# One quad of maxima in place of two, with its logits computed once and lowered by pixel between two turns

## The chip, the cores and the metric

The kernel runs on one core of one Trainium2 chip. The metric is the device time of one execution, in microseconds (us); a figure for a kernel is the median of its runs.

TensorE does matmuls, VectorE and GpSimd elementwise work, ScalarE exponentials and copies; DMA queues move data. PSUM is the memory that TensorE writes. This kernel uses it in tiles of two banks, called pairs, and three pairs rotate.

## The reference, cut to what matters

```python
def amm_conv3x3(x, centroids, w_sub, stride=1):          # a 3x3 convolution by code book
    p = ...                                                # (B, pixels, C, 9) patches
    d = sum(p*p) - 2.0 * einsum('bncs,cks->bnck', p, centroids) + sum(centroids**2)
    attn = softmax(-d, axis=-1)                            # over k = 16 codes of one channel
    lut = einsum('cks,cso->cko', centroids, w_sub)
    return einsum('bnck,cko->bno', attn, lut)
```

This runs twice for each of 16 images of 256 channels and 28 x 28 pixels. Group norm comes before it, batch norm and a squeeze-excite gate around it. A softmax doesn't change if the same number is taken from all 16 logits of a channel and pixel, and both kernels use this to keep the exponentials in range.

## The kernel before

The work of a layer and image is cut into 2 tiles of pixels (384 and 400) and 8 quads of 32 channels, so 16 slots. In each slot a group of **logits** (patches times codes), a group of **numerators** (exponentials times codes) and some **look-ups** (normalised numerators times weights, a full 128 x 128 matmul each) go to TensorE. Logits and numerators use small matmuls, 32 x 32 tiles of the array:

```python
def logits(u, rows):
    l, n = u["l"], u["px"][1]
    ps = [pair(), pair()]
    for t in range(4):
        for i in range(4):
            c = 32 * ctile(i, t)                     # (i + t) % 4
            nc.tensor.matmul(ps[t // 2][c : c + 32, t % 2, :n],
                lhsT=wd[l][32 * i : 32 * i + rows, 4 * u["m"] + t, :],
                rhs=u["pt"][32 * i : 32 * i + rows, t, :n], start=True, stop=True)
    return ps
```

The 16 matmuls (each leaves two records in the trace, 32 in all) go to 16 different tiles. Those of t = 0, 1 fill the first pair, those of t = 2, 3 the second. These are the two halves of a group.

The quads are sorted by how large their logits can get. In layer 2, quads 0 and 4 (`MAXED`) need the true maximum over the codes. They compute logits once to find it, then again with the maximum taken off. To turn means to transpose here; in the profile it is STREAM_TRANSPOSE:

```python
def a_turn(u):           # logits out of PSUM, turned so that codes lie along the free axis
    ...
def a_max(u, v):         # VectorE: maximum over 16 codes
    ...
def m_turn(u): ...       # turn the maxima, write them to DRAM (m_out), read them back as rows (m_in)
def b_logits(u):         # the logits again, with the maxima as more rows of the patches
    u["lg"] = logits(u, MROW + NCH if u["maxed"] else ONE + 1)
```

Each kernel is emitted in an order fixed by slot and position, and every engine works through its own part in that order. The positions within a slot:

```python
LOGITS, LOAD, MOVE, EXP, LOOK_A, NUM, TURN, SMALL, LOOK_B, MAX, LOOK_C, TURN_BACK, REST = range(13)
```

After the numerators VectorE turns them out of PSUM (`b_turn`) and takes the reciprocal, GpSimd normalises (`c_scale`), and VectorE turns the result back as `q` for the look-ups (`c_turn`, in TURN_BACK). A guard at the end checks the sums of exponentials and redoes the batch in a safe way if they leave a range.

## Time and profile before

| | before |
|---|---|
| time, median of 4 runs | 2812.78 us (2810.43 to 2818.25) |
| profiled execution | 2814.8 us, mean granted clock 0.990 |
| TensorE busy | 98% |
| VectorE / GpSimd / ScalarE busy | 80% / 63% / 39% |
| a round: a layer 1 and a layer 2 image, 32 slots | 169.21 us |

A busy share of 98% means less than it seems, since ends of matmuls are modelled. So I account for TensorE by starts: the time from the first record of a group to the start of the next thing. Over ten rounds in the middle of the run, per round:

| us per round | logits | numerators | look-ups | small matmuls | sum |
|---|---|---|---|---|---|
| before | 31.50 (36 groups) | 28.26 (32) | 108.18 | 1.28 | 169.21 |

### The profile page before, as it was taken

What the parts mean: (1) busy time and instruction counts of PE and PEld (TensorE: products, weight loads), DVE (VectorE), ACT (ScalarE), POOL (GpSimd) and SP (SyncE); (2) the same over time, 40 slices, a digit from 0 to 9 for tenths busy, and PEclk for the clock granted to TensorE, in tenths of its full rate; (3) what the DMA queues carried; (4) which work ended last, traced back from release to release, by engine and by line L of the source; (5) the groups of instructions that cost most, each with busy time, mean ns of one, the idle gap of its engine ahead of it and who ended that gap; (6) DMA issues with size and microseconds to landing.
All of it is one profiled execution on the core that took longest, in us unless ns stands there. A gap on an engine that the chain in (4) does not pass through costs nothing.

```text
span 2814.8 us, 94692 instructions
## 1 busy us (share of the span) xinstructions
PE 2756.0 (98%) x39794; PEld 1090.2 (39%) x39794; DVE 2252.0 (80%) x2772; ACT 1086.5 (39%) x1595; POOL 1782.1 (63%) x2589
## 2 busy tenths in 40 slices
PE   6999999999999999999999999999999999999996
PEld 3333333333333343333333333343333334333332
DVE  4668788887878878788887878878788887878885
ACT  2333433434334343433434334343433434334332
POOL 3785666756666575665756667575665756665653
PEclk9999999999999999999999999999999999999998
DMA  8787878768687676777777687676777767674641
GB/s 223 205 202 193 234 204 225 194 169 219 155 226 195 167 212 165 214 184 191 191 175 218 159 222 195 169 214 161 215 189 191 190 170 221 161 210 106 163 122 55
DMA packets 292787, 525.83 MB, mean 187 GB/s; under 512 B 94096, under 2 KB 247552, under 8 KB 292352
## 3 DMA queue, kind: packets, MB, share of 16 engines
q0 software_dynamic: 51808, 269.48, 36.0%
q1 hardware_dynamic: 240544, 250.20, 34.5%
q8 instruction: 315, 5.16, 0.8%
q14 instruction: 120, 0.98, 0.1%
HBM read 267.87 MB, written 251.69 MB: 185 GB/s over the span
## 4 chain that ended last, share of the span: by engine, by line
PE 92%; DVE 3%; POOL 2%; DMA 2%; issue 1%; ACT 0%; SPq 0%; DVEq 0%; POOLq 0%; ACTq 0%
PE acc L717 58%; PE pair L585 17%; PE pair L653 15%; DVE nt L665 1%; POOL k L681 1%; DMA pt<-pat 1%; DVE q L699 0%; DMA pat<-side 0%; DVE rc L671 0%; PE pair L319 0%; DMA out_dram<-y 0%; POOL pat L486 0%; PE pair L514 0%; POOL total L693 0%; DVE gn_st L434 0%
## 5 line engine op out<-in xcount | busy, mean ns | idle before, releaser
L717 PE MATMUL acc<-q,ws 128*128 128x384 f32 (+1 forms) x4096 | 1645.9, 520 | 5.1 <-ACT y L739 2.8
L681 POOL TENSOR_TENSOR k<-nt,rc 128x832 f32<-128x832 f32 (+1 forms) x512 | 802.9, 1568 | 980.6 <-DVE rc L671 970.7
L665 DVE STREAM_TRANSPOSE nt<-pair 128x832 f32<-128x832 f32 (+1 forms) x1024 | 979.3, 994 | 487.3 <-PE pair L653 436.0
L643 ACT ACTIVATE e<-pair 128x800 f32<-128x800 f32 (+1 forms) x1024 | 787.5, 821 | 1356.8 <-PE pair L585 1303.2
L717 PEld LDWEIGHTS acc<-q,ws 128*128 128x128 f32 x4096 | 698.1, 190 | 903.2 <-issue 577.6
L585 PE MATMUL pair<-pt,wd 19*32 19x384 f32 (+2 forms) x18432 | 556.6, 501 | 11.4 <-DMA pt<-pat 8.2
L699 DVE STREAM_TRANSPOSE q<-k 128x832 f32<-128x832 f32 (+1 forms) x512 | 488.9, 955 | 0.8 <-POOL k L681 0.8
L653 PE MATMUL pair<-e,cw 32*32 32x384 f32 (+1 forms) x16384 | 485.5, 501 | 0.3 <-DVE nt L665 0.2
L671 DVE RECIPROCAL rc<-nt 128x104 f32<-128x104 f32 (+1 forms) x512 | 398.5, 778 | 17.6
L585 PEld LDWEIGHTS pair<-pt,wd 19*32 19x32 f32 (+1 forms) x18432 | 138.2, 103 | 339.8 <-issue 276.2
L687 POOL TENSOR_TENSOR tail<-nt,rc 128x104 f32<-128x104 f32 (+1 forms) x512 | 236.7, 462 | 0.0
L653 PEld LDWEIGHTS pair<-e,cw 32*32 32x32 f32 x16384 | 119.9, 103 | 289.5 <-issue 154.8
L717 PE MATMUL acc<-qt,ws 128*128 128x400 f32 (+1 forms) x512 | 219.3, 510 | 0.0
L693 POOL TENSOR_TENSOR total<-total,nt 128x96 f32<-128x96 f32 (+1 forms) x448 | 197.4, 441 | 0.0
L486 POOL DMA_DIRECT2D pat<-side x274 | 184.7, 674 | 3.5 <-ACT side L475 3.0
L693 POOL TENSOR_TENSOR total<-total,rc 128x96 f32<-128x96 f32 (+1 forms) x448 | 176.1, 393 | 0.0
L717 PEld LDWEIGHTS acc<-qt,ws 128*128 128x128 f32 x512 | 91.1, 190 | 100.1 <-issue 50.3
L609 DVE TENSOR_REDUCE mx<-z 128x48 f32<-128x768 f32 (+1 forms) x128 | 120.6, 942 | 0.0
L604 DVE STREAM_TRANSPOSE z<-pair 128x768 f32<-128x768 f32 (+1 forms) x128 | 118.1, 961 | 0.0
L486 POOL DMA_DIRECT2D pat<-im x136 | 92.0, 677 | 0.7 <-ACT side L475 0.6
L739 ACT ACTIVATE y<-acc,bnsh,bnsc 128x384 f32<-128x384 f32 (+1 forms) x64 | 43.3, 677 | 87.3 <-PE acc L717 81.6
L551 POOL TENSOR_TENSOR y<-y,xt 128x392 f32<-128x392 f32 x60 | 65.9, 1099 | 10.4 <-ACT y L547 10.4
(113 smaller groups left out, 720.5 us busy)
## 6 DMA issues: line engine op xcount, KB each, us to landing
pat<-side POOLq DMA_DIRECT2D x232, 588.0 KB, 6.0
pt<-pat SPq DMA_DIRECT2D x1024, 112.5 KB
pt<-pat SPq DMA_DIRECT2D x1024, 108.0 KB
pat<-im POOLq DMA_DIRECT2D x116, 588.0 KB, 5.9
xt<-in_x POOLq DMA_DIRECT2D x32, 784.0 KB, 8.1
out_dram<-y POOLq DMA_DIRECT2D x16, 784.0 KB, 6.1
pat<-side POOLq DMA_DIRECT2D x24, 300.0 KB, 5.3
pat<-side POOLq DMA_DIRECT2D x18, 288.0 KB, 5.5
```

Source lines behind the costliest of these rows:

```text
L486: eng.dma_start(view(pat, (ROWS * p0 + 9 * k + 3 * dx) * HW + px, [[ROWS * HW, m], [HW, 3], [1, n]]), bass.AP(v.tensor, v.offset, [list(v. ...
L585: nc.tensor.matmul(ps[t // 2][c : c + 32, t % 2, :n], lhsT=wd[l][32 * i : 32 * i + rows, 4 * u["m"] + t, :], rhs=u["pt"][32 * i : 32 * i + ...
L609: nc.vector.tensor_reduce(u["mx"][:, 2 * v : 2 * v + 2].rearrange("p t (j b) -> p t b j", j=2)[:, :, :nb], u["z"].pop(0)[:, : 64 * nb].rea ...
L643: nc.scalar.activation(e[:, :, :n], ps[:, :, :n], AF.Exp, scale=2.0)
L653: nc.tensor.matmul(u["nm"][t // 2][32 * i : 32 * i + 32, t % 2, :n], lhsT=cw[l][c : c + 32, 4 * u["m"] + t, :], rhs=es[t // 2][c : c + 32, ...
L665: nc.vector.transpose(nt[:, :nb, 2 * v : 2 * v + 2].rearrange("p b t r -> p t b r"), ps[:, :, : 32 * nb].rearrange("p t (b r) -> p t b r", ...
L671: nc.vector.reciprocal(rc[:, : 8 * nb], u["nt"][:, :, SUM])
L681: nc.gpsimd.tensor_tensor(q[:, :nb].rearrange("p b (a s) -> p (b a) s", s=8), nt[:, :, :8], rc.unsqueeze(2).to_broadcast([P, 8 * nb, 8]), ...
L687: nc.gpsimd.tensor_tensor(tails[key][:, :nb, 8 * (m % 4) : 8 * (m % 4) + 8], nt[:, :, 8].rearrange("p (b a) -> p b a", a=8), rc.rearrange( ...
L693: nc.gpsimd.tensor_add(t[:, : 8 * nb], t[:, : 8 * nb], v)
L699: nc.vector.transpose(q[:, :, : 32 * nb].rearrange("p h (b r) -> p h b r", r=32), u.pop("k")[:, :nb].rearrange("p b (h r) -> p h b r", h=2),)
L717: nc.tensor.matmul(accs[key][:, :n], lhsT=ws[l][:, 2 * m + h if h < 2 else 2 * NQ + m // 4, o * P : (o + 1) * P], rhs=u["q"][h][:, :n], st ...
```

## The change

The intent: two quads with maxima become one, by taking from all codes of a channel a vector that brings them nearer to zero (in layer 2 alone, folded into the codes in the set-up, with the quads sorted anew). And that one quad computes its logits once: VectorE turns them out of PSUM and finds the maximum, GpSimd subtracts it, VectorE turns the result back, ScalarE takes the exponential from SBUF. The second logits group and the maxima's way through DRAM go.

```diff
-MAXED = (0, 4)
+MAXED = (0,)
... (new vector `bar`, codes less it, new sort: set-up only)
-    def m_turn(u): ...
-    def m_out(u): ...
-    def m_in(u): ...
-    def b_logits(u):
-        u["lg"] = logits(u, MROW + NCH if u["maxed"] else ONE + 1)
+    def a_less(u, v):
+        z, mx = by_code(u["z"][v]), u.pop(("mx", v))
+        nc.gpsimd.tensor_tensor(z, z, mx.unsqueeze(2).to_broadcast(list(z.shape)), ALU.subtract)
+    def a_back(u, v):
+        e = e_tile()
+        z = u["z"][v]
+        nc.vector.transpose(e[:, :, : 32 * blocks(u)], z.rearrange("p (t m) -> p t m", t=2))
+        u.setdefault("e", []).append(e)
+    def a_exp(u):
+        n = u["px"][1]
+        u.pop("z")
+        for e in u["e"]:
+            nc.scalar.activation(e[:, :, :n], e[:, :, :n], AF.Exp, scale=2.0)
... (in the plan; s is the slot of the quad with maxima, a = s - 5, where it was s - 6)
-                        at(a + 1, TURN_BACK, a_max, u, 0)
-                        at(a + 2, TURN_BACK, a_max, u, 1)
-                        at(a + 2, TURN_BACK, m_turn, u)
-                        at(a + 3, MOVE, m_out, u)
-                        at(a + 4, MOVE, m_in, u)
+                        for v in range(2):
+                            at(a + 1 + v, TURN_BACK, a_max, u, v)
+                            at(a + 2 + v, REST, a_less, u, v)
+                        at(s - 1, TURN_BACK, a_back, u, 0)
+                        at(s, EXP, a_back, u, 1)
+                        at(s, EXP, a_exp, u)
                     else:
...
-                    at(s, LOGITS, b_logits, u)
-                    at(s, EXP, b_exp, u)
+                        at(s, LOGITS, logits, u)
+                        at(s, EXP, b_exp, u)
```

I call one such quad of one pixel tile a unit. There are 32 units in the changed kernel, two per image.

More of the change, by code (lines that the diff above doesn't have):

```diff
@@ L35 @@
 ONE = ROWS
-MROW = ONE + 1
 SUM = 9
 PXT = ((0, 384), (384, 400))
-MAXED = (0, 4)
+MAXED = (0,)
+LEAN = 0.2
 REACH = 5.0
-SHIFT = (0.0, 35.0)
+SHIFT = 25.0
 def chan(rt, j):
@@ L83 @@
     nhalf: bass.AP,
-    mones: bass.AP,
     consts: bass.AP,
@@ L112 @@
     dram = ctx.enter_context(tc.tile_pool(name="dram", bufs=1, space=DRAM))
-    drot = ctx.enter_context(tc.tile_pool(name="drot", bufs=3, space=DRAM))
     small = ctx.enter_context(tc.tile_pool(name="small", bufs=3))
@@ L175 @@
     wd = [load(wd1, "wd0"), const.tile([P, NT, 32], F32, name="wd1")]
-    mones_sb = const.tile([P, 2, 32], F32, name="mones_sb")
-    nc.sync.dma_start(mones_sb, mones.rearrange("l p m -> p l m"))
     pts = [const.tile([P, 4, 400], F32, name=f"pt{i}") for i in range(6)]
@@ L220 @@
         nc.vector.memset(t[:, :, 400:416], 1.0)
-    mxs = [const.tile([P, 4, 32], F32, name=f"mx{i}") for i in range(2)]
-    for t in mxs:
-        nc.vector.memset(t, 0.0)
     totals = [const.tile([P, 13 * 8], F32, name=f"total{i}") for i in range(2)]
@@ L253, in scratch, with lessen_codes @@
         return kpool.tile([P, 13, 64], F32, tag="k", name="scratch").rearrange("p i m -> p (i m)")[:, :n]
+    bar = const.tile([P, NB, 9], F32, name="bar")
+    c2_less = const.tile([P, NB, 10 * K], F32, name="c2_less")
+    def lessen_codes():
+        less = c2_less.rearrange("p b (s k) -> p b s k", k=K)
+        for b in range(NB):
+            nc.vector.tensor_sub(
+                less[:, b, :9], c2_sb[:, b].rearrange("p (k s) -> p s k", s=9), bar[:, b].unsqueeze(2).to_broadcast([P, 9, K])
+            )
+        sq = scratch(NB * K * 9)
+        nc.vector.tensor_mul(sq, c2_sb.rearrange("p b m -> p (b m)"), c2_sb.rearrange("p b m -> p (b m)"))
+        nc.vector.tensor_reduce(less[:, :, 9], sq.rearrange("p (b k s) -> p b k s", b=NB, s=9), axis=AX.X, op=ALU.add)
+        nc.vector.tensor_scalar(less[:, :, 9], less[:, :, 9], -0.5, -SHIFT / 2, op0=ALU.mult, op1=ALU.add)
     def sort_keys():
@@ L257, in sort_keys @@
         key = small.tile([P, NB], F32, name="key")
-        pos = scratch(NB * K * 9)
-        nc.vector.tensor_scalar_max(pos, c2_sb.rearrange("p b m -> p (b m)"), 0.0)
-        sums = small.tile([P, NB * K], F32, name="sums")
-        nc.vector.tensor_reduce(sums, pos.rearrange("p (m s) -> p m s", s=9), axis=AX.X, op=ALU.add)
-        nc.vector.tensor_reduce(key, sums.rearrange("p (b k) -> p b k", k=K), axis=AX.X, op=ALU.max)
+        by_tap = c2_sb.rearrange("p b (k s) -> p b s k", s=9)
+        mean, way = (small.tile([P, NB, 9], F32, name=f"c2_{v}") for v in ("mean", "way"))
+        nc.vector.tensor_reduce(mean, by_tap, axis=AX.X, op=ALU.add)
+        nc.vector.tensor_reduce(way, by_tap, axis=AX.X, op=ALU.max)
+        nc.vector.tensor_scalar_mul(mean, mean, 1.0 / K)
+        nc.vector.tensor_sub(way, way, mean)
+        nc.vector.tensor_reduce(key, way, axis=AX.X, op=ALU.add)
+        nc.vector.scalar_tensor_tensor(bar, way, LEAN, mean, op0=ALU.mult, op1=ALU.add)
         t = small.tile([P, NB], F32, name="key_t")
@@ L274, in sort_keys @@
             nc.tensor.matmul(ps[:, b * P : (b + 1) * P], lhsT=ones_sq, rhs=dg, start=True, stop=True)
-        row = epool.tile([P, 2, 400], F32, tag="e", name="row")[:, 0, :C]
+        row = epool.tile([P, 2, 416], F32, tag="e", name="row")[:, 0, :C]
         nc.vector.tensor_copy(row, ps[:, :C])
@@ L326, in sort_ws1, with by_position @@
                 nc.scalar.copy(w, ps[:, :C])
-    d_c2 = [dram.tile([C, K * 9], F32, name=f"dc2{i}") for i in range(2)]
-    def by_position(ps, rhs, m):
+    d_c2 = [dram.tile([C, m], F32, name=f"dc2{i}") for i, m in enumerate((9 * K, 10 * K))]
+    def by_position(ps, rhs):
         for v in range(NB):
@@ L333, in by_position @@
                 nc.tensor.matmul(
-                    ps[:, v, :m], lhsT=perm[:, b, v * P : (v + 1) * P], rhs=rhs[:, b], start=(b == 0), stop=(b == NB - 1)
+                    ps[:, v], lhsT=perm[:, b, v * P : (v + 1) * P], rhs=rhs[:, b], start=(b == 0), stop=(b == NB - 1)
                 )
@@ L339, in sort_c2 @@
         ps = pair()
-        by_position(ps, c2_sb, K * 9)
-        for i in range(2):
-            t = scratch(NB * K * 9).rearrange("p (b m) -> p b m", b=NB)
-            if i == 0:
-                nc.scalar.copy(t, ps[:, :, : K * 9])
-            else:
-                nc.scalar.copy(
-                    t.rearrange("p b (s k) -> p b s k", k=K), ps[:, :, : K * 9].rearrange("p b (k s) -> p b s k", s=9)
-                )
-            nc.gpsimd.dma_start(view(d_c2[i], 0, [[K * 9, P], [P * K * 9, NB], [1, K * 9]]), t)
+        m0 = 0
+        for d, rhs in zip(d_c2, (c2_sb, c2_less)):
+            m = rhs.shape[2]
+            by_position(ps[:, :, m0 : m0 + m], rhs)
+            t = scratch(NB * m).rearrange("p (b m) -> p b m", b=NB)
+            nc.scalar.copy(t, ps[:, :, m0 : m0 + m])
+            nc.gpsimd.dma_start(view(d, 0, [[m, P], [P * m, NB], [1, m]]), t)
+            m0 += m
     def place_wd2(j, s):
-        m = K * 9
+        m = 10 * K
         nc.sync.dma_start(
-            wd[1][prow(j, s) :: 32, :, K * j : K * j + K],
+            wd[1][prow(j, s) if s < 9 else ONE :: 32, :, K * j : K * j + K],
             view(d_c2[1], NRT * j * m + s * K, [[m, 4], [4 * m, NT], [1, K]]),
@@ L400, with square_codes @@
     squares = []
-    def square_codes(l):
-        wf = wd[l].rearrange("p t m -> p (t m)")
+    def square_codes():
+        wf = wd[0].rearrange("p t m -> p (t m)")
         for c0 in range(0, NT * 32, 384):
@@ L408, in square_codes, with setup_codes @@
             squares.append((c0, n, sq))
-    def setup_codes(l):
-        wf = wd[l].rearrange("p t m -> p (t m)")
+    def setup_codes():
+        wf = wd[0].rearrange("p t m -> p (t m)")
         for c0, n, sq in squares:
@@ L415, in setup_codes @@
             nc.vector.tensor_add(wf[:, c0 : c0 + n], wf[:, c0 : c0 + n], ps[:, :n])
-        squares.clear()
-        nc.vector.tensor_add(wd[l], wd[l], mones_sb[:, l].unsqueeze(1).to_broadcast([P, NT, 32]))
     tpool = ctx.enter_context(tc.tile_pool(name="tpool", bufs=3))
@@ L560, in store @@
             d.pop(b)
-    maxed = [0]
     def patches(u, tile):
@@ L567, in patches @@
         pt = pts[tile]
-        if u["maxed"]:
-            u["mx"] = mxs[maxed[0] % 2]
-            maxed[0] += 1
         for i in range(4):
@@ L576, in patches, with logits @@
         u["pt"] = pt
-    def logits(u, rows):
+    def logits(u):
+        rows = ONE + 1
         l, n = u["l"], u["px"][1]
@@ L590, in logits @@
                 )
-        return ps
+        u["lg"] = ps
     def blocks(u):
         return (u["px"][1] + 31) // 32
-    def a_logits(u):
-        u["lg"] = logits(u, ONE + 1)
     def a_turn(u):
@@ L604, in a_turn, with by_code, e_tile @@
             nc.vector.transpose(z[:, : 64 * nb].rearrange("p (t m) -> p t m", t=2), ps[:, :, : 32 * nb])
-            u["z"].append(z)
+            u["z"].append(z[:, : 64 * nb])
+    def by_code(z):
+        return z.rearrange("p (g k) -> p g k", k=K)
     def a_max(u, v):
-        nb = blocks(u)
-        nc.vector.tensor_reduce(
-            u["mx"][:, 2 * v : 2 * v + 2].rearrange("p t (j b) -> p t b j", j=2)[:, :, :nb],
-            u["z"].pop(0)[:, : 64 * nb].rearrange("p (t b j k) -> p t b j k", t=2, j=2, k=K),
-            axis=AX.X, op=ALU.max,
-        )
-    def m_turn(u):
-        mt = small.tile([P, 4, 32], F32, name="mt")
-        nc.vector.transpose(mt.rearrange("p a b -> p (a b)"), u["mx"].rearrange("p a b -> p (a b)"))
-        u["mt"] = mt
-    def m_out(u):
-        d = drot.tile([4 * 256, 32], F32, tag="dm", name="dm")
-        for p0, n in ((0, P), (P, 96)):
-            nc.sync.dma_start(view(d, 32 * p0, [[32, n], [256 * 32, 4], [1, 32]]), u["mt"][:n])
-        u["dm"] = d
-    def m_in(u):
-        n = u["px"][1]
-        for j in range(NCH):
-            nc.sync.dma_start(
-                u["pt"][MROW + j :: 32, :, :n],
-                view(u["dm"], j * 512, [[1024, 4], [256 * 32 + 1024, 4], [1, n]]),
-            )
-    def b_logits(u):
-        u["lg"] = logits(u, MROW + NCH if u["maxed"] else ONE + 1)
+        mx = small.tile([P, 52], F32, name="mx")[:, : 4 * blocks(u)]
+        nc.vector.tensor_reduce(mx, by_code(u["z"][v]), axis=AX.X, op=ALU.max)
+        u["mx", v] = mx
+    def a_less(u, v):
+        z, mx = by_code(u["z"][v]), u.pop(("mx", v))
+        nc.gpsimd.tensor_tensor(z, z, mx.unsqueeze(2).to_broadcast(list(z.shape)), ALU.subtract)
+    def e_tile():
+        return epool.tile([P, 2, 416], F32, tag="e", name="e")
+    def a_back(u, v):
[4 more added lines that the diff above has]
+    def a_exp(u):
+        n = u["px"][1]
+        u.pop("z")
+        for e in u["e"]:
+            nc.scalar.activation(e[:, :, :n], e[:, :, :n], AF.Exp, scale=2.0)
     def b_exp(u):
@@ L641, in b_exp @@
         for ps in u.pop("lg"):
-            e = epool.tile([P, 2, 400], F32, tag="e", name="e")
+            e = e_tile()
             nc.scalar.activation(e[:, :, :n], ps[:, :, :n], AF.Exp, scale=2.0)
@@ L797, in stage @@
                         a = s - self.lb
-                        self.loads.append((a - self.lead, s, u))
-                        at(a, MAX, a_logits, u)
+                        self.loads.append((a - self.lead, a, u))
+                        at(a, MAX, logits, u)
                         at(a, MAX, a_turn, u)
-                        at(a + 1, TURN_BACK, a_max, u, 0)
-                        at(a + 2, TURN_BACK, a_max, u, 1)
-                        at(a + 2, TURN_BACK, m_turn, u)
-                        at(a + 3, MOVE, m_out, u)
-                        at(a + 4, MOVE, m_in, u)
+                        for v in range(2):
[4 more added lines that the diff above has]
+                        at(s, EXP, a_exp, u)
                     else:
                         self.loads.append((s - self.lead, s, u))
-                    at(s, LOGITS, b_logits, u)
-                    at(s, EXP, b_exp, u)
+                        at(s, LOGITS, logits, u)
+                        at(s, EXP, b_exp, u)
                     at(s + 1, NUM, b_num, u)
@@ L869 @@
     row = sort_keys()
-    square_codes(0)
+    square_codes()
     for k in range(NB):
@@ L876 @@
     sort_ranks(row)
-    setup_codes(0)
+    setup_codes()
     for k in range(NB):
@@ L884 @@
     sort_bn()
-    plan = Plan(1, 3, 6)
+    lessen_codes()
+    plan = Plan(1, 3, 5)
     for si, (l, b) in enumerate(stages):
@@ L915 @@
         plan.at(6 + g, REST, fetch_ws2, g)
-    for i, (j, s) in enumerate((j, s) for j in range(NCH) for s in range(9)):
+    for i, (j, s) in enumerate((j, s) for j in range(NCH) for s in range(10)):
         plan.at(6 + i // 3, REST, place_wd2, j, s)
@@ L919 @@
         plan.at(12 + i // 2, REST, place_cw2, c, t, j)
-    plan.at(14, REST, square_codes, 1)
-    plan.at(15, REST, setup_codes, 1)
     plan.emit()
@@ L939 @@
             load_x("g", x[bass.ds(bi, 1)].rearrange("o c n -> (o c) n"))
-            plan = Plan(8, 3, 6)
+            plan = Plan(8, 3, 5)
             plan.norm("g", 4)
@@ L1008, in _lay_out @@
     nhalf = np.zeros((P, P), np.float32)
-    mones = np.zeros((2, P, 32), np.float32)
     for i in range(4):
         nhalf[32 * i : 32 * i + 32, 32 * i + ONE] = -0.5
-        for j in range(NCH):
-            mones[:, 32 * i + MROW + j, K * j : K * j + K] = -1.0
-        for l in range(2):
-            mones[l, 32 * i + ONE] = -SHIFT[l] / 2
-    arrays["in_nhalf"], arrays["in_mones"] = nhalf, mones
+    arrays["in_nhalf"] = nhalf
     arrays["in_consts"] = np.ones((1, HW), np.float32)
```

## The prediction

> **What bounds the kernel now.** I read the page first (busy shares, slices, chain, groups), then TensorE's instructions in order of time in the middle of the run, then VectorE's beside them, then the last 80 us.
>
> ```profile
> span 2814.8 us, 94692 instructions
> ...
> PE 2756.0 (98%) x39794; PEld 1090.2 (39%) x39794; DVE 2252.0 (80%) x2772; ACT 1086.5 (39%) x1595; POOL 1782.1 (63%) x2589
> ...
> PE acc L717 58%; PE pair L585 17%; PE pair L653 15%; DVE nt L665 1%; POOL k L681 1%; DMA pt<-pat 1%; DVE q L699 0%; DMA pat<-side 0%; DVE rc L671 0%; PE pair L319 0%; DMA out_dram<-y 0%; POOL pat L486 0%; PE pair L514 0%; POOL total L693 0%; DVE gn_st L434 0%
> ...
> L585 PE MATMUL pair<-pt,wd 19*32 19x384 f32 (+2 forms) x18432 | 556.6, 501 | 11.4 <-DMA pt<-pat 8.2
> ...
> L609 DVE TENSOR_REDUCE mx<-z 128x48 f32<-128x768 f32 (+1 forms) x128 | 120.6, 942 | 0.0
> L604 DVE STREAM_TRANSPOSE z<-pair 128x768 f32<-128x768 f32 (+1 forms) x128 | 118.1, 961 | 0.0
> ```
>
> The chain that ended last is TensorE for 90% in three lines: look-ups (L717), logits (L585), numerators (L653). The work comes in 512 slots (16 images x 2 layers x 2 pixel tiles x 8 quads), and one group of logits is 32 records: 18432/32 = 576 groups. The 64 above 512 are what layer 2 computes twice: 4 quads with maxima per image. A busy TensorE may still have holes, since ends are modelled, so I used start-to-start distances. TensorE in order of time, where one of those extra groups sits:
>
> ```profile
> 1218.03 0.93 PE L585 MATMUL pair<-pt,wd 19*32 19x384 f32 x32
> 1218.89 1.56 PE L717 MATMUL acc<-q,ws 128*128 128x384 f32 x4
> 1220.38 1.10 PE L585 MATMUL pair<-pt,wd 19*32 19x400 f32 x32
> 1221.40 0.91 PE L717 MATMUL acc<-q,ws 128*128 128x384 f32 x2
> 1222.15 0.81 PE L717 MATMUL acc<-qt,ws 128*128 128x384 f32 x2
> ```
>
> A logits group takes 0.86 us (384 pixels; 0.885 for 400 elsewhere), and look-ups follow without a hole. The same slot of two neighbouring rounds, 1147.23 and 1316.44, gives 169.21 us for a layer-1 and a layer-2 image. Nominal: 2 x (16 groups x 0.86 + 36 look-ups x 0.743) + 2 x (16 x 0.885 + 36 x 0.77) + 4 extra groups (3.5) + about 1.35 of small matmuls = 169.6. So the middle is pure TensorE time, with nothing to hide an added wait in.
>
> **What the Trainium skill says.** "Perfetto Trace Analysis", Identifying the Most-Contended Engine, calls matmul busy time a bad measure; the nominal sum is why I trust it here. The same page, Tensor Engine Instruction, says "ACT/DVE/GPSIMD are strict FIFO": new VectorE work put ahead of a numerator turn delays it. The end of the run below agrees. "SBUF — State Buffer", Who interferes with whom, says a VectorE instruction with at most one SBUF input doesn't contend with GpSimd: turns and maxima should not be slowed by the new subtractions. The trace agrees: q's turn keeps 0.92 to 0.99 us beside GpSimd's k. "TensorEngine Tiling (Array Packing)", PSUM Bottleneck, warns that packing speeds TensorE but not the emptying of PSUM. That is the risk here: three PSUM pairs rotate, and VectorE empties the numerators.
>
> **The change, part by part.** Only 2 instead of 4 units per layer-2 image keep a maximum (32 in all), and they compute logits once.
>
> Removed: 64 extra logits groups, 32 of 0.86 and 32 of 0.885 = 55.8 us of TensorE, all on the path. On VectorE 64 turns out of PSUM, 64 maxima and 64 small turns (0.31) = 61 + 60 + 20 = 141 us; the maxima's trip through DRAM; the set-up of layer 2's codes (TensorE 1.9 us at 137.6, plus a VectorE wait of 1.1).
>
> Added: 64 turns back from SBUF (as q's turn, 0.92/0.99: 61 us, so VectorE nets -80); 64 subtractions on GpSimd (as k, 1.51/1.62: 100 us) and 64 more sums for the guard (0.42: 27), so GpSimd goes from 63% to about 69%, beside TensorE; in the set-up a few VectorE operations (about 1 us more before the sort), four more matmuls, and two more small transfers for the codes. The exponentials stay, now from SBUF. I put the set-up at 0 +- 2 us. Had the guard fired, the whole batch would be redone; I recomputed the sums of exponentials for the new sort from the inputs, and they stay between 7e-21 and 1.4e26, inside 1e-26 and 1e32.
>
> What may come back: where the turns back land. In the slot of such a unit there is no logits group any more, so the slot is short for TensorE, and VectorE's queue has both turns back before the next numerator turn. First an ordinary VectorE round, with idle time before the turns:
>
> ```profile
> 1176.80 1.85 DVE L665 STREAM_TRANSPOSE nt<-pair 128x768 f32<-128x768 f32 x2 [0.77 <-PE pair L653]
> 1178.68 0.75 DVE L671 RECIPROCAL rc<-nt 128x96 f32<-128x96 f32 x1
> 1179.35 0.92 DVE L699 STREAM_TRANSPOSE q<-k 128x768 f32<-128x768 f32 x1
> 1182.26 1.85 DVE L665 STREAM_TRANSPOSE nt<-pair 128x768 f32<-128x768 f32 x2 [2.00 <-PE pair L653]
> ```
>
> Time zero is the start of a numerator group (1175.74 there). Turns start at 1.06, q's turn at 3.61, done at 4.45 by spacing. With two turns back of 832 (0.91 spacing, from q's turn of that size) the next numerator turn can start at 6.27. TensorE, by the order of the built kernel: numerators 0.86, two look-ups 1.49, (no logits), two look-ups 1.49, so the next numerators start at 3.84 and end at 4.70; two look-ups to 6.19; then the next logits. Their first half goes to a free pair, until 6.63; their second half needs the pair that the late turn empties. From a turn's start to such a half I read 1.02 us, from the one place where the kernel before does this, at its end:
>
> ```profile
> 2733.93 2.67 DVE L543 SCALAR_TENSOR_TENSOR y<-xt,gn_rstd,y 128x392 f32<-128x392 f32 x4
> ...
> 2735.65 0.90 PE L585 MATMUL pair<-pt,wd 19*32 19x400 f32 x16
> ...
> 2736.53 1.83 DVE L665 STREAM_TRANSPOSE nt<-pair 128x768 f32<-128x768 f32 x2
> ...
> 2737.55 0.91 PE L585 MATMUL pair<-pt,wd 19*32 19x400 f32 x16 [1.00 <-DVE nt L665]
> ```
>
> There four VectorE operations held the turn, and the group broke in two halves. In the changed kernel the second half starts at about 6.27 + 1.02 = 7.3 instead of 6.63: 0.7 us lost. The tile's other unit (q's turn of 832, turns back of 768, one look-up more before and one fewer after) comes to 7.5 against 6.8: again 0.7. 32 units x 0.7 = 22 us, with an uncertainty of 0.3 to 1.1 each. After it VectorE catches up within one slot (the next numerators are 5.9 us later), so the delay doesn't spread.
>
> At the end of the run the first tile of the last image waits for the store of the image before:
>
> ```profile
> 2747.41 9.16 DMA out_dram<-y
> ```
>
> TensorE gets there about 1.8 us earlier, VectorE's chain about 0.8: I count 1 us as lost. Sum: 2811.7 - 55.8 + 22.4 + 1 + 0.5 (set-up) = 2780.
>
> **The rivals.** (1) No wait comes: the whole 55.8 us is kept, 2757. For it: VectorE's total falls by 80 us to about 77%, and the first turn back could run as early as GpSimd lets it. Against it: the order puts both between q's turn and the numerator turn, and 0.7 us follows even with each at its spacing. (2) VectorE or the PSUM pairs bind harder, 1.2 us per unit or more, with the maxima's rounds also late: 2795 to 2800. For it: a round with q's turn, the tail's turn and a maximum ends at about 6.2 us against 5.9. Against it: the logits after it need the pair only 0.45 us later still. (3) GpSimd becomes the bound: two slots with 2.85 + 1.55 + 0.68 (a transfer's issue) = 5.1 us against 4.85 to 5.6; its results are needed a slot later (3 us of slack), so no time. (4) Less small DMA speeds the run: the 94096 packets under 512 bytes get fewer, but TensorE waits for pixel loads only 8.2 us in all, in the first 130 us, so a few us at most, against two more transfers there.
>
> **Range and chances.** The saving is firm to 1 or 2 us; the wait is the uncertain term, 10 to 38 us. So 2780, 8 in 10 between 2759 and 2797. Faster by over 2% needs below 2755.5, that is no wait at all and luck in the set-up: 0.08. Slower by over 2% needs 110 us of waits, or the guard firing: 0.01. The rest, 0.91, is within 2%.
>
> **What would show it.** Logits records fall to 16384 and their group by some 62 us. Two-image rounds shrink from 169.2 to about 167.1. Right after each unit of maxima the logits group of the following slot lies in two halves of 16 records, released by the numerator turn, the group then taking about 1.6 us; the idle time printed there will be smaller than 0.7, since the modelled end of the first half lies 0.45 late. TensorE's chain still carries 90%. GpSimd at about 69%, VectorE near 77 to 78%. If the halves are not split, rival 1 holds and rounds are 165.7; if the numerators or the maxima's rounds are split too, rival 2.

## The result, and the profile after

| | before | after |
|---|---|---|
| median | 2812.78 us (2810.43 to 2818.25, 4 runs) | 2786.59 us (2784.22 to 2790.07, 4 runs) |
| ratio, with 95% interval | | 0.9905 (0.9887 to 0.9923) |
| profiled execution | 2814.8 us | 2782.7 us |
| round | 169.21 us | 167.41 us |

A ratio here is always the mean time of one kernel's runs over the mean of the runs of before from the same rounds, so it is not quite the ratio of the medians. The two profiled executions lie 32.1 us apart, the medians 26.2; I use the first to say where time went and the second for how much.

The page of the changed kernel: span, busy shares, the chain that ended last, and the group of logits (busy us, mean ns of one; then idle time ahead and its releaser):

```profile
span 2782.7 us, 90173 instructions
...
PE 2706.4 (97%) x37748; PEld 1081.3 (39%) x37748; DVE 2180.1 (78%) x2645; ACT 1093.1 (39%) x1595; POOL 1902.7 (68%) x2714
...
PE acc L717 54%; PE pair L591 15%; PE pair L653 14%; DVE nt L665 3%; DVE q L699 1%; DVE rc L671 1%; DVE e L629 1%; POOL k L681 1%; DMA pat<-side 0%; POOL pat L496 0%; POOL total L693 0%; PE pair L333 0%; DMA pt<-pat 0%; PE pair L524 0%; DVE gn_st L444 0%
...
L591 PE MATMUL pair<-pt,wd 19*32 19x384 f32 (+1 forms) x16384 | 519.4, 501 | 27.4 <-DVE nt L665 17.2
```

Logits records fell from 18432 to 16384. TensorE's three lines still make the chain, but it now passes through VectorE: the numerator turn (L665), the reciprocal (L671) and the new turn back (L629). The logits group names the numerator turn as what it waits for. The 64 subtractions on GpSimd (z, from z and mx) took 99.0 us in all, as reckoned (100).

The timeline behind a unit, the answer to the round and the broken group that the prediction showed of before (start, length, engine, line, operation; in brackets the idle time ahead):

```profile
1273.65 0.93 PE L653 MATMUL pair<-e,cw 32*32 32x384 f32 x32
...
1277.28 0.93 PE L653 MATMUL pair<-e,cw 32*32 32x384 f32 x32
1278.10 1.92 DVE L629 STREAM_TRANSPOSE e<-z 128x832 f32<-128x832 f32 x2
...
1279.63 0.90 PE L591 MATMUL pair<-pt,wd 19*32 19x400 f32 x16
1279.94 1.81 DVE L665 STREAM_TRANSPOSE nt<-pair 128x768 f32<-128x768 f32 x2
1280.94 0.91 PE L591 MATMUL pair<-pt,wd 19*32 19x400 f32 x16 [0.41 <-DVE nt L665]
1281.77 2.20 PE L717 MATMUL acc<-q,ws 128*128 128x384 f32 x6
...
1286.28 0.95 PE L591 MATMUL pair<-pt,wd 19*32 19x400 f32 x32
1287.16 1.56 PE L717 MATMUL acc<-q,ws 128*128 128x384 f32 x4
```

VectorE does the two turns back (1278.10), and only then the numerator turn (1279.94). TensorE needs a pair that this turn empties, so the logits group lies in halves of 16. The brackets say 0.41 us idle. The group's real cost is read from starts: 1279.63 to 1281.77 is 2.14 us, where a whole group takes 0.885 (1286.28 to 1287.16, rounded). So a unit loses 1.255 us, three times the printed idle time.

The busy records of this group in windows of 0.05 us show why. The columns are the window, its length, TensorE's busy time with the number of records, the same of weight loads, granted clock, DMA share, GB/s. First the split group's two halves, then a whole group of the same size at 1286.28:

```profile
1279.85:1279.90 0.05, 0.05 (x8) 0.00 (x0) 1.00 1.21 251
1281.15:1281.20 0.05, 0.05 (x8) 0.00 (x0) 1.00 1.69 251
1286.50:1286.55 0.05, 0.05 (x16) 0.01 (x2) 1.00 0.62 128
```

A half of a split group runs 8 records at a time, in two waves, so it takes 0.83 us alone (1280.94 to 1281.77). A whole group runs 16 at a time and takes 0.885 for both halves. **The halves run side by side, not one after the other**: the difference, 0.885 - 0.83 = 0.055 us, is how late the second may start at no cost.

All 32 units are split: 28 groups take 2.11 to 2.15 us, three 2.5, and the last 5.44 (2703.21 to 2708.65), since VectorE's finish of the previous image stands between its two turns back. Its second half also runs at a granted clock of 0.50 (in a window over 2707.13 to 2708.65), so that it takes 1.52 us instead of 0.83:

```profile
2702.59 2.66 DVE L553 SCALAR_TENSOR_TENSOR y<-xt,gn_rstd,y 128x392 f32<-128x392 f32 x4
2703.21 0.90 PE L591 MATMUL pair<-pt,wd 19*32 19x400 f32 x16
...
2707.13 1.59 PE L591 MATMUL pair<-pt,wd 19*32 19x400 f32 x16 [3.03 <-DVE nt L665]
```

### The profile page after: what moved, and what is told of

Same layout as the page of the kernel before. It is cut to its first block, busy times and chain, and to the rows that moved or that the text cites.

```text
span 2782.7 us, 90173 instructions
## 1 busy us (share of the span) xinstructions
PE 2706.4 (97%) x37748; PEld 1081.3 (39%) x37748; DVE 2180.1 (78%) x2645; ACT 1093.1 (39%) x1595; POOL 1902.7 (68%) x2714
## 2 busy tenths in 40 slices
DMA packets 230825, 514.99 MB, mean 185 GB/s; under 512 B 34184, under 2 KB 185608, under 8 KB 230408
## 4 chain that ended last, share of the span: by engine, by line
PE 85%; DVE 8%; issue 3%; POOL 2%; DMA 1%; ACT 0%; SPq 0%; DVEq 0%; POOLq 0%; ACTq 0%
PE acc L717 54%; PE pair L591 15%; PE pair L653 14%; DVE nt L665 3%; DVE q L699 1%; DVE rc L671 1%; DVE e L629 1%; POOL k L681 1%; DMA pat<-side 0%; POOL pat L496 0%; POOL total L693 0%; PE pair L333 0%; DMA pt<-pat 0%; PE pair L524 0%; DVE gn_st L444 0%
## 5 line engine op out<-in xcount | busy, mean ns | idle before, releaser
L665 DVE STREAM_TRANSPOSE nt<-pair 128x832 f32<-128x832 f32 (+1 forms) x1024 | 978.3, 993 | 528.2 <-PE pair L653 441.0
L643 ACT ACTIVATE e<-pair 128x768 f32<-128x768 f32 (+1 forms) x960 | 740.2, 821 | 1045.2 <-PE pair L591 1044.5
L591 PE MATMUL pair<-pt,wd 19*32 19x384 f32 (+1 forms) x16384 | 519.4, 501 | 27.4 <-DVE nt L665 17.2
L671 DVE RECIPROCAL rc<-nt 128x104 f32<-128x104 f32 (+1 forms) x512 | 398.7, 779 | 17.6
L591 PEld LDWEIGHTS pair<-pt,wd 19*32 19x32 f32 x16384 | 125.5, 103 | 341.0 <-issue 241.7
L687 POOL TENSOR_TENSOR tail<-nt,rc 128x104 f32<-128x104 f32 (+1 forms) x512 | 243.1, 475 | 0.0
L693 POOL TENSOR_TENSOR total<-total,nt 128x96 f32<-128x96 f32 (+1 forms) x480 | 213.3, 444 | 0.0
L693 POOL TENSOR_TENSOR total<-total,rc 128x96 f32<-128x96 f32 (+1 forms) x480 | 188.1, 392 | 0.0
L636 ACT ACTIVATE e<-e 128x768 f32<-128x768 f32 (+1 forms) x64 | 54.9, 857 | 191.1 <-DVE e L629 190.0
L729 ACT ACTIVATE im<-acc,bnsh,bnsc 128x384 f32<-128x384 f32 (+1 forms) x64 | 43.4, 679 | 149.6 <-PE acc L717 139.4
L621 POOL TENSOR_TENSOR z<-z,mx 128x768 f32<-128x768 f32 (+1 forms) x64 | 99.0, 1546 | 0.0
```

The costliest lines, as they stand in the source:

```text
L591: nc.tensor.matmul(ps[t // 2][c : c + 32, t % 2, :n], lhsT=wd[l][32 * i : 32 * i + rows, 4 * u["m"] + t, :], rhs=u["pt"][32 * i : 32 * i + ...
L621: nc.gpsimd.tensor_tensor(z, z, mx.unsqueeze(2).to_broadcast(list(z.shape)), ALU.subtract)
L643: nc.scalar.activation(e[:, :, :n], ps[:, :, :n], AF.Exp, scale=2.0)
L665: nc.vector.transpose(nt[:, :nb, 2 * v : 2 * v + 2].rearrange("p b t r -> p t b r"), ps[:, :, : 32 * nb].rearrange("p t (b r) -> p t b r", ...
L671: nc.vector.reciprocal(rc[:, : 8 * nb], u["nt"][:, :, SUM])
L687: nc.gpsimd.tensor_tensor(tails[key][:, :nb, 8 * (m % 4) : 8 * (m % 4) + 8], nt[:, :, 8].rearrange("p (b a) -> p b a", a=8), rc.rearrange( ...
```

## The experiments

Nine kernels ran; every one gave a correct result. The first four share 11 runs of before (median 2815.13 us, 2810.19 to 2823.57), the next four 35 (2813.90, 2810.20 to 2822.85), the last 7 (2813.26, 2806.64 to 2820.25). The accounts per round are by starts, over the same ten rounds:

| kernel | median us | ratio to before (95%) | round | logits | numerators | look-ups |
|---|---|---|---|---|---|---|
| after | 2786.59 | 0.9905 (0.9887 to 0.9923) | 167.41 | 30.49 | 28.26 | 107.40 |
| e1: turns back a slot earlier | 2754.80 | 0.9783 (0.9766 to 0.9800) | 165.42 | 28.48 | 28.28 | 107.39 |
| e2: second turn back twice | 2842.08 | 1.0096 (1.0080 to 1.0111) | 170.66 | 32.74 | 28.26 | 108.38 |
| e3: two more look-ups ahead | 2745.09 | 0.9749 (0.9732 to 0.9766) | 164.89 | 27.96 | 28.27 | 107.39 |
| e4: one quad, logits still twice | 2776.82 | 0.9867 (0.9846 to 0.9888) | 167.08 | 29.75 | 28.27 | 107.78 |
| e5: second turn back later | 2817.11 | 1.0014 (1.0007 to 1.0020) | 169.45 | 28.67 | 32.09 | 107.42 |
| e6: e1 and e3 | 2743.14 | 0.9753 (0.9740 to 0.9766) | 164.83 | 27.91 | 28.26 | 107.39 |
| e7: one more look-up ahead | 2765.31 | 0.9834 (0.9821 to 0.9846) | 166.09 | 29.15 | 28.27 | 107.40 |
| e8: second turn back one and a half times | 2813.51 | 0.9999 (0.9989 to 1.0008) | 169.15 | 31.74 | 28.30 | 107.84 |
| e9: e2 and e3 | 2777.85 | 0.9871 (0.9849 to 0.9892) | 166.86 | 29.92 | 28.27 | 107.40 |

My theory was that the late numerator turn, held by the two turns back, costs what the sum lacks of 55.8 us. The rivals were that something else does: load on GpSimd or VectorE, or the way through SBUF itself.

### e1: both turns back one slot earlier

```diff
-        e = e_tile()
+        e = tpool.tile([P, 832], F32, tag="z", name="eb").rearrange("p (t m) -> p t m", t=2)
...
-                        at(s - 1, TURN_BACK, a_back, u, 0)
-                        at(s, EXP, a_back, u, 1)
+                        at(s - 2, TURN_BACK, a_back, u, 0)
+                        at(s - 1, TURN_BACK, a_back, u, 1)
```

> The changed kernel with each turn back one slot earlier (the first two slots before the unit's own, the second one slot before), written to a tile of the pool of z, so that no buffer of the exponentials is held longer. Theory A (the wait comes from both turns back standing directly before one numerator turn in a short slot): by the same working the numerator turn can start at 5.4 us instead of 6.29 after the zero point, so the second half of the next logits starts at 6.4, when TensorE gets there (6.42): the 32 split logits groups vanish and about 31 us with them, 2755 to 2758 us, 0.98 of before, rounds of 165.6 us. Rival B (VectorE simply has too much work around these units, wherever it stands, or the exponentials from SBUF are late): the waits move to other groups and the time stays at 2780 to 2790.

Measured: 2754.80 us, at the edge of what the theory gave, though 0.28 us per unit that it didn't foresee stays. All the added work is still there; only its place differs, and no more than one turn back now stands ahead of a numerator turn. The groups behind a unit lost their clear split and take 1.14 to 1.19 us instead of 2.14. The timeline of e1:

```profile
1268.95 1.80 DVE L665 STREAM_TRANSPOSE nt<-pair 128x768 f32<-128x768 f32 x2
1269.64 1.22 PE L591 MATMUL pair<-pt,wd 19*32 19x400 f32 x32
1270.78 2.20 PE L717 MATMUL acc<-q,ws 128*128 128x384 f32 x6
```

The numerator turn now starts ahead of the logits, by 0.69 us, where it started 0.31 after them (1279.63, 1279.94). From a turn's start to the half that it releases is 1.00 us, so the second half can start at 1269.95; due at 1269.64 + 0.055, it comes 0.25 late. That is about what is seen.

### e2: the second turn back done twice

```diff
-        nc.vector.transpose(e[:, :, : 32 * blocks(u)], z.rearrange("p (t m) -> p t m", t=2))
+        for _ in range(1 + v):
+            nc.vector.transpose(e[:, :, : 32 * blocks(u)], z.rearrange("p (t m) -> p t m", t=2))
```

> The changed kernel with the second turn back done twice (the same data to the same place, so the result is right). Theory A: each of the 32 waits grows by one spacing of such a turn, 0.85 to 0.91 us, so the second halves start 2.2 us after the first instead of 1.31, and the time grows by 28 us to about 2814. Rival B2 (the wait has another last cause, such as the exponentials or GpSimd's subtraction, and the turn back only stands beside it): less than 10 us more.

Measured: 2842.08 us, 55 more than the changed kernel. Two things make it up. The groups behind a unit take mostly 3.12 to 3.23 us, 1.0 to 1.1 more, so about 33 us: VectorE's delay goes to the end undiminished (its three turns take 2.93 us up to the numerator turn, where two take 1.84). The rest was a surprise. The windows of e2 (2 us each: busy times of TensorE, weight loads, VectorE, ScalarE and GpSimd, then the granted clock, the DMA share and GB/s):

```profile
966.00:968.00 2.00, 2.00 (x18) 0.57 (x3) 1.97 (x3) 1.92 (x3) 0.59 (x1) 0.50 0.95 329
968.00:970.00 2.00, 2.00 (x6) 1.06 (x4) 0.16 (x1) 0.16 (x1) 2.00 (x5) 0.66 0.82 303
```

Right behind the wait (a hole of 1.49 us, ended at 965.73) the granted clock, 1.00 in the windows ahead and again from 970, is 0.50 for some 3.4 us, and six look-up records that take 2.2 us elsewhere took 3.29. This happened behind 13 of the 31 waits of about 1.5 us (not "most", as the expectation of e8 says), and behind the last one, of 4.09. It cost about 1.7 us each time, for the 13 together 22 us. The Trainium skill, "TensorE: Matmul & The Clock Gate", Part 1, describes a clock that goes to half after a window of about 3.4 us in which the array idles, the windows running free of the program. The half clock and the length agree with this trace, and so do windows that run free: by its clock records the 13 falls start whole multiples of 3.413 us apart (from 580.24 to 795.28 are 63). On this grid all 13 holes hit began 0.3 to 1.7 us into a step, and the 18 spared began 1.8 us in or later. But the hole is shorter than the page's window, and how much idle time within one it takes was not measured.

### e3: the turns back unmoved, two more look-ups ahead of the waiting logits

```diff
-                more = [2 if (s, MAX) in self.jobs else 0 for s in slots]
+                more = [2 if (s, MAX) in self.jobs or ((s, EXP) in self.jobs and (s, LOGITS) not in self.jobs) else 0 for s in slots]
```

> The changed kernel with the turns back where they are, but two more look-ups of TensorE in the slot that has no logits group (the other slots of the tile give them up). Theory A: TensorE reaches the second half of the next logits 1.49 us later, at 7.9 against 7.3 when the pair is free, so the groups are not split and the time falls by some 28 us to 2756 to 2760. Rival B (VectorE's work itself is too much): the work of both engines is the same as in the changed kernel, so the time stays at 2780 to 2790.

Measured: 2745.09 us, 2.5% faster than before, and 11 us below the range expected, since more was lost per unit than the 0.87 us then reckoned. No group in the steady part is split. VectorE's order is that of the changed kernel, and so is its load; TensorE merely has other work until the turn is done. The timeline of e3:

```profile
1261.85 2.85 PE L717 MATMUL acc<-q,ws 128*128 128x384 f32 x8
1263.65 1.80 DVE L665 STREAM_TRANSPOSE nt<-pair 128x768 f32<-128x768 f32 x2
1264.62 0.95 PE L591 MATMUL pair<-pt,wd 19*32 19x400 f32 x32
```

The logits start 0.97 us after the turn, and the turn's 1.00 us are nearly over. With e1 this settles that the late numerator turn is the cause: it is removed by moving either side of it. The rivals fall, since VectorE, GpSimd and the way through SBUF do the same work here.

### e4: one quad with maxima, but logits twice and maxima through DRAM

```diff
... (new codes and sort kept; the maxima's path of before put back)
-                        at(s - 1, TURN_BACK, a_back, u, 0)
-                        at(s, EXP, a_back, u, 1)
-                        at(s, EXP, a_exp, u)
+                        at(a + 2, TURN_BACK, m_turn, u)
+                        at(a + 3, MOVE, m_out, u)
+                        at(a + 4, MOVE, m_in, u)
...
+                    at(s, LOGITS, b_logits, u)
+                    at(s, EXP, b_exp, u)
```

> Half of the change alone: the new codes and sort, one quad instead of two with maxima, but the logits of such a quad computed twice and the maxima sent through DRAM, as in the kernel before. 32 extra logits groups of 0.86 to 0.885 us stay, no turns back. Theory A: 2812.8 - 27.9 (32 groups less) - 2 to 3 (set-up) = 2782 to 2785, the same as the whole change within 5 us: computing the logits once wins 27.9 us and loses about 31 to its wait. Rival (fewer quads also shorten something else, or the trip through DRAM costs time): more than 8 us away from the changed kernel.

Measured: 2776.82 us, 10 us *less* than the whole change. This misses the range expected and lies just past the 8 us that were to speak for the rival; by the accounts the wait was under-reckoned (40 us, not 31), and the look-ups take 0.40 us less per round. So as placed, the second part of the change (logits computed once) loses: it takes 32 groups away, about 28 us, and brings some 40 of waits. The first part (one quad instead of two) is the whole gain. With the turns' wait removed (e3, 2745.09 us) the second part gains some 32 us on top.

### e5: the second turn back and the exponentials behind the numerator turn

```diff
-                        at(s, EXP, a_back, u, 1)
-                        at(s, EXP, a_exp, u)
+                        at(s, TURN, a_back, u, 1)
+                        at(s, TURN, a_exp, u)
```

> As the changed kernel, but the second turn back and the exponentials of a unit of maxima come after the numerator turn and the reciprocal of their slot on VectorE, not ahead of them. Time zero is the start of the slot's numerators. The numerator turn can now start 0.9 us earlier, so the logits group of the next slot should be whole again. But the second half of the unit's own numerators, due 8.8 us after zero, needs the second half's exponential: turn at 5.4 to 7.2, reciprocal to 7.95, turn back to 8.85, exponential (0.86, measured) to about 9.75. My theory (VectorE's queue is one line, and whatever is last in it makes TensorE wait): the wait moves from the logits to the numerators, about 1.0 us for each of 32 units, and the time stays at 2786, within 6; the numerator groups after a unit lie in halves of 16, with ScalarE named as releaser. Rival (only a late numerator turn matters, the exponentials have room): no split at all and 2755 to 2760. A third outcome, the numerators split and the time above 2795, would say that the exponential is later than I reckon.

Measured: 2817.11 us, the third outcome, with the wait moved to the numerators. The timeline of e5 at one of 31 such waits (32.6 us of printed idle time in all):

```profile
1295.35 0.87 ACT L636 ACTIVATE e<-e 128x800 f32<-128x800 f32 x1 [2.55 <-DVE e L629]
1295.70 0.90 PE L653 MATMUL pair<-e,cw 32*32 32x400 f32 x16
1296.12 0.81 ACT L487 COPY side<-im 128x756 f32<-128x756 f32 x1
1296.84 1.56 ACT L643 ACTIVATE e<-pair 128x800 f32<-128x800 f32 x2
1297.72 0.91 PE L653 MATMUL pair<-e,cw 32*32 32x400 f32 x16 [1.12 <-ACT e L643]
```

The unit's second exponential comes at 1295.35, which is 8.98 us after zero and ends at 9.85, about as reckoned (9.75); so it is not late, as I had read this outcome beforehand. But the releaser is another one, the exponential at 1296.84 of the ordinary logits behind it. It frees the pair that the numerators' second half writes, and in ScalarE's line it stands behind the late exponential and a copy. So the delay of one result held an engine, and the engine held a buffer. The split numerator groups take 2.7 to 2.86 us, and 0.36 us stay at the logits.

### e6: e1 and e3 together

The edit is the two diffs together.

> The two remedies together: turns back a slot earlier each and two more look-ups in the slot without logits. Each alone took the splits away (2754.8 and 2745.1 in the first set). If what remains is TensorE's own time without holes, two remedies give no more than the better of them: 2742 to 2747, rounds of two images 164.8 again. If the look-ups alone still hid a wait at VectorE that the profile does not show, both together are faster by another 4 us or more: 2741 or less in both median and mean of rounds. At the end of the run the 1.7 us wait before the last image's half group should be gone, which is worth 1.7 us at most.

Measured: 2743.14 us and a round of 164.83, against 164.89 in e3. The two can't be told apart, so nothing of this wait is left in the steady part. At the end 0.7 us of the last image's wait is printed, where e3 has 1.7.

### e7: one more look-up instead of two

```diff
-                more = [2 if (s, MAX) in self.jobs else 0 for s in slots]
+                more = [2 if (s, MAX) in self.jobs else 1 if (s, EXP) in self.jobs and (s, LOGITS) not in self.jobs else 0 for s in slots]
```

> Only one more look-up in the slot without logits, where two were enough. One look-up is 0.74 us, the wait of the changed kernel 0.87 us for each of 28 of the 32 units. If that wait is a plain difference of two arrival times, about 0.1 us stays of each (32 x 0.1 = 3 to 5 us above the kernel with two more look-ups): 2747 to 2752, with groups after a unit of about 1.0 us instead of 0.88. If a wait, once it comes, costs a fixed amount whatever its length, the groups stay in clear halves and the time is 2765 or more.

Measured: 2765.31 us: the outcome that I had put down to a wait of fixed cost, and not the 2747 to 2752 of my own reckoning. The timeline of e7:

```profile
1273.14 1.80 DVE L665 STREAM_TRANSPOSE nt<-pair 128x768 f32<-128x768 f32 x2
1273.47 1.57 PE L591 MATMUL pair<-pt,wd 19*32 19x400 f32 x32
1274.97 2.20 PE L717 MATMUL acc<-q,ws 128*128 128x384 f32 x6
```

The group prints as one of 32 records with no idle time, yet takes 1.50 us. A third look-up in a run of three takes 0.64 us (at 384 columns a run of four records takes 1.49, of six 2.13). So with a loss of 1.255 in the changed kernel, 1.255 - 0.64 = 0.61 should stay with one more look-up, and none with two (1.28). The groups of e7 take 1.44 to 1.50, so 0.58 to 0.62 stay. No fixed cost is needed: the second half is simply due 0.055 us after the first starts.

### e8: half of the second turn back repeated

```diff
-        nc.vector.transpose(e[:, :, : 32 * blocks(u)], z.rearrange("p (t m) -> p t m", t=2))
+        for k in range(2, 1 - v, -1):
+            nc.vector.transpose(e[:, :k, : 32 * blocks(u)], z.rearrange("p (t m) -> p t m", t=2)[:, :k])
```

> As the changed kernel, with half of the second turn back done a second time (half of its columns, about 0.5 us more of VectorE ahead of the numerator turn). With a whole turn repeated the wait grew from 0.87 to about 1.9 us, and after most of those waits the look-ups ran at a granted clock of 0.50 for some 3 us, about 1.65 us lost again per round of two images. If the clock falls only beyond some length of wait between 0.9 and 1.9 us, this wait of about 1.4 us shows on which side it lies: without a fall 32 x 0.5 = 16 us more than the changed kernel, 2802 (2799 to 2806), mean granted clock near 0.99; with it 2812 to 2829 and a mean clock near 0.98. If VectorE's delay were partly hidden, less than 2799.

Measured: 2813.51 us, in the lower part of what I gave for a falling clock. The groups take 2.72 to 2.80 us, 0.6 more than in the changed kernel, 19 us together. The clock fell behind 3 of the units' waits in the middle (holes of 1.05 us) and once at the end, as in the changed kernel; one such place in e8:

```profile
957.98 0.91 PE L591 MATMUL pair<-pt,wd 19*32 19x400 f32 x16 [1.05 <-DVE nt L666]
958.81 3.90 PE L718 MATMUL acc<-q,ws 128*128 128x384 f32 x6
```

So there is no sharp length. In the profiled runs the fall came behind 13 of 31 holes of about 1.5 us, 3 of 31 of 1.05, none of 30 of 1.03 to 1.12 at e5's numerators, and none of the 31 of 0.41 to 0.78 in the changed kernel. Of the 30.6 us between the two profiled executions, starts give 20.9 to the logits groups and 8.3 to the look-ups, 5 of these to the three falls. The 14 runs of e8 go from 2807.60 us at a mean clock of 0.991 to 2819.64 at 0.985, so the falls seem to differ in number from run to run.

### e9: e2 and e3 together, to test the rule ahead of time

> The second turn back done twice and two more look-ups in the slot without logits, together. A test ahead of time of a rule that I formed after the runs before it: the two halves of a logits group occupy different tiles of the array and run side by side, so the second half is due 0.055 us after the first starts, not 0.44 us after it. Then a unit of maxima costs the changed kernel 1.255 us (group 2.14 instead of 0.885), the second turn done twice adds 1.04, and two more look-ups take off 2 x 0.64 = 1.28: 1.0 us stays per unit, the groups after a unit take 1.88 to 1.92 us from their start to the next look-up, a round of two images takes 166.9, and the time is 2745 + 32 x 1.0 = 2777 (2773 to 2782). By the rule of the prediction (halves one after the other, a wait of 0.87 in the changed kernel) 0.87 + 1.04 - 1.28 = 0.63 us would stay, the groups would take 1.5 us and the time would be 2765 (2762 to 2768). The hole on TensorE is some 0.2 us, as short as in the changed kernel, so the granted clock should not fall after it: mean clock 0.99.

Measured: 2777.85 us, where the rule of side-by-side halves said 2777 and the rule of the prediction 2765. The round is 166.86 (expected 166.9). The groups take 1.78 us (384 pixels) and 1.94 (400), on both sides of the 1.88 to 1.92 expected, so 0.92 and 1.05 stay, mean 0.99. The clock didn't fall behind them, with a hole of 0.20. The timeline of e9:

```profile
1281.11 0.90 PE L591 MATMUL pair<-pt,wd 19*32 19x400 f32 x16
1282.21 0.90 PE L591 MATMUL pair<-pt,wd 19*32 19x400 f32 x16 [0.20 <-DVE nt L666]
1283.05 1.56 PE L718 MATMUL acc<-q,ws 128*128 128x384 f32 x4
```

## Why the prediction was right, and where it was not

The time was predicted as 2780, within 2759 to 2797, and came out at 2786.59, with "within 2%" at 0.91. The mechanism was named and came as named. Two terms of the sum were wrong by much, and they nearly cancelled.

- **Logits removed, 55.8 us: right.** Per round 31.50 became 27.96 in e3, which has no waits: 3.54, and over 16 rounds 56.6 us.
- **The wait of 0.7 us per unit, 22.4 us in all: right in kind and place, too small.** It measured 1.255 us in 28 units and more in four: per round 30.49 - 27.96 = 2.53, so 40 us over 16 rounds. The step that failed reads "Their first half goes to a free pair, until 6.63; their second half needs the pair that the late turn empties." It takes the halves as following each other, with the second due 0.44 us after the first. They run side by side, so it was due at 0.055, which gives 0.39 us more per unit. The Trainium skill has it: "TensorEngine Tiling (Array Packing)", Key Properties, says that tiles operate independently and can run in parallel. The windows of 0.05 us agree, with 16 records at a time against 8. I had read the page only for its PSUM warning. The other 0.2 us is TensorE coming earlier: the next numerators start 3.63 us after zero instead of 3.84, and the logits at 5.98 instead of 6.19. The four look-ups ahead of those numerators now run in one piece and take 2.77 us, not 2 x 1.49.
- **VectorE's times in that sum: right.** The numerator turn was put at 6.27 after zero and came at 6.29; the second half was put at 7.3 and came at 7.29.
- **Look-ups unchanged: wrong, and not seen as a term at all.** They take 0.78 us less per round with the same number of records, 12.5 us over 16 rounds. A look-up behind a tiled group costs about 0.75 us and so does the next, but each further one in the same run only 0.64: at 384 columns runs of four records take 1.49, of six 2.13, of eight 2.78 (at 400 columns 1.54, 2.21, 2.88). Where a logits group goes, two runs become one. The same page and section say that a change of tiling mode drains TensorE. This trace agrees in sign and puts it at about 0.2 us per run. What exactly takes that time was not isolated.
- **The set-up and the end, +1.5 us: not resolved.** In the profiled runs what is left is 32.1 - (56.6 - 40.5 + 12.5) = 3.5 us of gain, but starts of profiled kernels differ among themselves by that much.

The sum of what was measured is -56.6 + 40.5 - 12.5 - 3.5 = -32.1 us between the profiled executions, against -31.9 predicted. So the centre was partly luck: an error of 18 us up and one of 12 down. The two are tied in part: about half of the look-ups' gain (32 times 0.2 us) lies right ahead of a unit's wait, and only made that wait longer.

The rivals: (1) no wait at all, 2757, did not hold for this kernel but is what e1 and e3 make of it. In (2) the size was right per unit (1.2 us or more), but the maxima's rounds stayed whole. (3) GpSimd at 68% cost nothing, and q's turn beside it kept its mean (955 ns before, 954 after), as the prediction took from "SBUF — State Buffer" (the page excepts the 2-port modes, which the prediction left out). (4) Packets under 512 bytes fell from 94096 to 34184, and no gain from this is seen.

Of the signs named beforehand, the halves of 16, the releaser, the round (167.1 predicted, 167.41 measured), GpSimd and VectorE's share came. Wrong were the split group's length (1.6 predicted, 2.14 measured), the fall of the logits group's busy time (62 predicted, 37.2 measured, as split halves count as busy) and the share of TensorE's three lines in the chain (90% predicted, 83% measured).

## What to carry to other kernels

Work that leaves a full engine pays only if what it adds elsewhere doesn't stand ahead of something that the full engine needs: look at the order on the other engine, and move either side. Here two look-ups moved by one line turned 0.9905 into 0.9749. When a wait lands inside a group of packed matmuls, reckon its cost from the start of the whole group to the start of the next one: the printed idle time, 0.41 us here, was a third of the loss.

## What the Trainium skill lacked or had wrong

- "TensorE: Matmul & The Clock Gate", Why this matters for your kernels, asks for no idle gaps over about 3 us to keep the clock up. Here it fell to 0.50, for some 3.4 us and a loss of about 1.7 us, behind 13 of 31 holes of about 1.5 us (e2) and 3 of 31 of 1.05 us (e8). Where Part 1 of the page speaks of shorter idle times, it gives no length. The array ran only half of its tiles on both sides of each hole, which may count; no run here separates that.
- No page says what a wait inside a packed group costs. Here the part ahead of it and the part behind each take almost the time of the whole (0.83 us for half, 0.885 for all), so a hole of 0.41 us cost 1.255.
- "TensorEngine Tiling (Array Packing)" says that a change of tiling mode drains TensorE, without a size. Here a run of two look-ups between tiled groups takes 1.49 us, and each further one 0.64 (384 columns), so about 0.2 us per run goes to its first two.
- "Perfetto Trace Analysis" warns of TensorE's busy time, but no page says that a half-used array prints as busy: a group of 32 records printed without idle time (e7) took 1.50 us instead of 0.885.
